# Routing in a fused decoder layer: its first two parts behind the mix and behind the next reciprocal, the ranking for blank entries at the heads of steps

## The chip, the cores and the metric

The kernel runs on one core of a Trainium2 chip. A core has five engines, each with an in-order queue of its own: TensorE (PE in the profile; PEld is its loading of weights), VectorE (DVE), ScalarE (ACT), GpSimd (POOL) and SyncE (SP, which here issues DMAs). They work side by side and wait for each other by semaphores. The metric is the device time of one execution in microseconds; of several runs the median is taken.

## The reference

The reference computes a decoder layer on 16 sequences of 128 rows of 256 numbers, in float32, and has three parts, each on a layer-normalised input and added to it.

```python
x = x + _L0_attn_ref(_layernorm(x), ...)                    # causal attention, 16 heads, latent size 72
x = x + _L0_xattn_ref(_layernorm(x), ctx, ctx, w, u)        # bidirectional decaying sums over ctx, gated by sigmoid(x)
x = x + _L0_ffn_ref(_layernorm(x), router_w, w_gate, w_up, w_down)   # 8 experts, two of them for each row
```

What matters here is how the third part chooses its experts for a row:

```python
logits = x @ router_w.T                     # 8 numbers a row
m1, ind1 = max(scores), argmax(scores)      # the best expert
m2, ind2 = the same with ind1 masked        # the second best
mult1, mult2 = softmax over those within the jitter threshold, at ind1 and ind2
out += dense_w[:, e] * ((silu(x @ w_gate[e].T) * (x @ w_up[e].T)) @ w_down[e].T)   # for each e
```

## The kernel before, in words

**Two halves.** The first 64 steps do attention, gating and routing; a step is one unit, four of the 16 heads of one sequence, so that a sequence `b` begins at step 4b. After them come 36 slots (`turn`, `up` L1033, `down` L1058, `add` L1071), each of which takes 128 listed rows through one expert; some of the slots stand under a condition. A slot gathers its rows by a list and adds its result into the output with an indirect DMA.

**A step.** The loop at the end of the function writes out the order of the work by hand: `scores` of unit s (L465) on TensorE; `normalize` of unit s-1, which is the reciprocal of the sums on VectorE (L502) and the product on GpSimd (L503); what the plan has for the place "pre"; `turn_probs` of unit s-2, four transposes on TensorE (L509) and a copy by ScalarE (L511); place "A"; `maxima` of unit s on VectorE (L482), its four exponentials on ScalarE (L490) and `lay_mask`, which writes the mask into the bank of scores that step s+2 will use (L477); the query tiles of the next pair of sequences (L427, with their copies by ScalarE L433 further down); place "B"; `values` (L517) and their copies (L529, L532); places "C" and "D". Within a place, what was entered first comes first. All engines are fed from this one order, each with its own share of it, and `ctx.enter_context(tc.manual_schedule())` keeps it as written.

**The plan.** `at(step, place, function, ...)` enters a piece of work. For each sequence it holds, beside others: `wkv_exps` (ScalarE L556 and L558, GpSimd L559 and L560), the two decaying sums (VectorE L568 and L585, with additions on GpSimd L580 and L590), `project` (TensorE L543), `residual` (VectorE L596), `mix_1` and `mix_2` (VectorE L625, the reciprocal L630 of 128x256, the product L631, then GpSimd's addition L632), the statistics of the mixed rows (L328, L329, L321, GpSimd L323), the normalised row (ScalarE L648), and the logits (TensorE L675, copied by VectorE L687). For most sequences the mix stands at place "B" of step 4b+9.

**PSUM.** Transposes share two banks under the tag "t": those of the probabilities L509, of the gating sums L621 (which the mix reads, L631 last), of rows and of latents. Query tiles, logits, the ranking of routing and the small products of the blank entries share two banks under "mm". A bank is free again when its last reader is done.

**Routing.** `route(r)` handles four sequences at once and is a generator; each `route_part` runs it to its next `yield`. The first part makes absolute values (VectorE L704) and finds the best expert (L707 a maximum, L709 and L710, L711 a maximum, L712, then L714 to mask it); the second part finds the second best by the same five instructions L707 to L712. The third takes the differences (L717 to L722, with an exponential on ScalarE, L723). The fourth ranks rows among those of the same expert by matmuls on TensorE (L728 to L731) and makes the gates (L739 to L741); the fifth makes the places (L754 to L765). The scatters of entries into lists by GpSimd (L771) follow.

**Blank entries.** For the first four sequences alone, `strangers` runs between the fifth part and the scatters. Its six parts are: two small VectorE instructions (L787, L788), two comparisons of 128x1024 (L793, a part for each), sixteen small matmuls on TensorE with their copy (L804, L808), a transpose with its copy (L812, L813), and a DMA by SP (L815). Entries of `lists` that no row takes have to name rows that are not of this expert, and this part finds them.

**Tables.** `first_table` counts the rows of each expert and makes a list of slots. Its first part is a product on TensorE (L823) and five small VectorE instructions (L825 to L835).

Of the kernel before, what the change touches and what calls it, by code (L numbers as in the profile page):

```python
# [19 lines left out]
B = 16  # L20
T = 128
N = B * T
C = 256
# [55 lines left out]
def decoder_kernel(  # L79
# [1004 lines left out]
    def at(step, place, fn, *args):  # L1084
        plan.setdefault((step, place), []).append((fn, args))
# [107 lines left out]
    for b in range(B):  # L1193
        s = NHG * b
        if b + 1 < B:
            at(s + 2, "pre", load_ctx, b + 1)
        at(s + 1, "C", wkv_exps, b)
        at(s + 2, "B", wkv_back, b)
        at(s + 3, "A", wkv_back_add, b)
        at(s + 4, "B", wkv_forth, b)  # L1200
        at(s + 5, "A", wkv_forth_add, b)
        at(s + 5, "B", project, b, (0, 1))
        at(s + 6, "B", project, b, (2, 3))
        at(s + 6, "C", rest_values, b)
        at(s + 7, "B", project, b, (4, 5))
        at(s + 7, "C" if b < B - 1 else "B", project, b, (6, 7, NP))
        for name, (step, place) in {B - 2: last_but_one, B - 1: last}.get(b, usual).items():
            at(s + step, place, stages[name], b)
        if b < E:
            for k in range(3):  # L1210
                at(s + 11 + k, "C", load_expert, b, k)
        if b % RB == RB - 1:
            r = b // RB
            parts = ((13, "B"), (13, "C"), (14, "B"), (15, "B"), (15, "C"))
            if b == B - 1:
                parts = ((12, "B"), (12, "D"), (13, "B"), (13, "D"), (14, "B"))
            for step, place in parts:
                at(s + step, place, route_part, r)
            if r == 0:
                for step, place in ((16, "B"), (16, "C"), (17, "B"), (17, "C"), (18, "C"), (19, "B")):  # L1220
                    at(s + step, place, route_part, r)
            for k in range(2 * RB):
                if b < B - 1:
                    at(s + (20 if r == 0 else 16) + k, "A", route_part, r)
                else:
                    at(s + 14 + (k + 1) // 3, "CDA"[(k + 2) % 3 if k > 1 else k], route_part, r)
        if b + 1 in FIRST_B:
            i = FIRST_B.index(b + 1)
            parts = [(19 + k, "C") for k in range(6)]
            if i:  # L1230
                parts = [(18, "C"), (20, "D"), (21, "B"), (21, "D"), (22, "D"), (23, "D")]
            for step, place in parts:
                at(s + step, place, table_part, i, first_table, i)
            for k in range(0, S1[i], 2):
                at(s + 24 + k // 2, "C", list_slots, min(2, S1[i] - k))
        if b == B - 1:
            for k in range(5):
                at(s + 15 + k // 3, "ABD"[k % 3], table_part, "2", last_table)
            for k in range(0, S2, 4):
                at(s + 17 + k // 4, "C", list_slots, min(4, S2 - k))  # L1240
# [153 lines left out]
```

## Time and profile before

| | |
|---|---|
| median of 3 runs | 553.93 us (552.38 to 557.51) |
| the profiled execution | 551.19 us |
| its span in the profile | 549.4 us |
| mean granted clock of TensorE | 0.989 |
| busy share of the span: PE, DVE, ACT, POOL | 93%, 60%, 60%, 60% |

The span runs from the first to the last instruction of the profiled execution; the rest of its time lies around it. The busy shares are averages over two halves that differ: in the steps all four engines have work, in the slots nearly everything waits for TensorE. A row of the timeline has the start in us, the duration in us, the engine, the line, the operation, what is written from what, the sizes and the number of instructions; in brackets stands how long the engine had been idle and whose end released it. A row of stretches has the bounds in us, the length, the busy time of PE, PEld, DVE, ACT and POOL with the number of instructions, the granted clock, the busy share of the DMA engines and GB/s.

### The profile page before, as it was taken

To read this page: it belongs to the slowest core of one execution; us is meant where nothing else is said; L and a number is where in the kernel's file an instruction comes from. 1 tells how busy PE (TensorE), PEld (TensorE's weight loads), DVE (VectorE), ACT (ScalarE), POOL (GpSimd) and SP (SyncE) were. 2 spreads that over 40 slices of the span, in tenths; PEclk is the share of its full clock that TensorE was granted. 3 is DMA by queue.
4 is the path that set the end of the run, shared out by engine and by line. 5 is a ranking of instruction groups with operands and counts; after the bars stand their busy time and mean duration, and the time that the engine had idled before them with its cause. 6 is when DMAs were issued, how large, how long until landed. Compare 5 with 4: busy or idle time off the path is not lost. (4 is left out here: it accounts for less than half of the span.)

```text
span 549.4 us, 10171 instructions
## 1 busy us (share of the span) xinstructions
PE 512.7 (93%) x3289; PEld 438.4 (80%) x3289; DVE 330.0 (60%) x811; ACT 329.3 (60%) x953; POOL 330.9 (60%) x386
## 2 busy tenths in 40 slices
PE   4999999999989999999998989999989999998991
PEld 3778788877768876887875769989979999997991
DVE  2345676677986687888859867565654333333320
ACT  1788998898788897888887873523422222222210
POOL 5456656574576985687655895555685454543522
PEclk9899999999999999999998999999999999999997
DMA  5422255363453555222131122233223423232221
GB/s 150 110 79 69 66 143 175 115 192 125 109 182 118 157 142 158 81 69 67 32 100 36 52 55 55 49 61 45 43 39 53 59 41 56 41 53 47 39 30 19
DMA packets 39632, 45.51 MB, mean 83 GB/s; under 512 B 14129, under 2 KB 31410, under 8 KB 39578
## 3 DMA queue, kind: packets, MB, share of 16 engines
q1 hardware_dynamic: 30076, 35.12, 22.5%
q0 software_dynamic: 7936, 9.51, 11.3%
q8 instruction: 28, 0.46, 0.4%
q10 hardware_dynamic: 1566, 0.21, 0.2%
q14 instruction: 26, 0.21, 0.2%
HBM read 26.12 MB, written 11.23 MB: 68 GB/s over the span
## 5 line engine op out<-in xcount | busy, mean ns | idle before, releaser
L1071 POOL DMA_INDIRECT out_dram<-y,en x36 | 62.0, 1724 | 78.9 <-DVE y L1069 54.6
L490 ACT ACTIVATE pr<-s,nm 128x128 f32<-128x128 f32 x256 | 90.7, 370 | 11.4 <-DVE nm L482 11.3
L503 POOL TENSOR_TENSOR pr<-pr,rsum 128x512 f32<-128x512 f32 x64 | 75.7, 1183 | 36.0 <-DVE rsum L502 23.8
L1046 ACT ACTIVATE sl<-s 128x512 f32<-128x512 f32 x36 | 21.5, 597 | 119.0 <-PE s L1033 107.3
L465 PEld LDWEIGHTS s<-kvT,q 72*128 72x128 f32 x512 | 65.8, 192 | 16.6 <-issue 12.1
L1033 PEld LDWEIGHTS s<-xT,w 128*128 128x128 f32 x576 | 69.2, 192 | 9.5 <-issue 6.8
L1033 PE MATMUL s<-xT,w 128*128 128x128 f32 x576 | 70.8, 276 | 5.1 <-DVEq L1019 2.0
L543 PE MATMUL po<-outw_sb,yP 128*128 128x256 f32 x288 | 74.1, 385 | 0.7 <-DMA yP<-yd 0.7
L465 PE MATMUL s<-kvT,q 72*128 72x128 f32 x512 | 70.2, 279 | 1.9 <-DMA q<-qr 1.7
L1048 DVE TENSOR_TENSOR hT<-sl,pu 128x512 f32<-128x512 f32 x36 | 24.7, 687 | 76.2 <-PE pu L1033 57.1
L1033 PE MATMUL pu<-xT,w 128*128 128x128 f32 x576 | 70.2, 275 | 0.0
L1058 PE MATMUL pd<-wall,hT 128*128 x288 | 68.2, 380 | 0.8 <-DVE hT L1048 0.8
L517 PE MATMUL py<-aT,kvN 128*72 128x512 f32 x128 | 66.3, 600 | 1.6 <-ACT aT L511 1.3
L1033 PEld LDWEIGHTS pu<-xT,w 128*128 128x128 f32 x576 | 67.3, 192 | 0.1
L427 PE MATMUL pq<-xnT,wq_sb 128*128 128x256 f32 x256 | 65.8, 389 | 0.6 <-DVE found L808 0.6
L543 PEld LDWEIGHTS po<-outw_sb,yP 128*128 128x128 f32 x288 | 54.1, 193 | 12.7 <-issue 5.2
L482 DVE TENSOR_REDUCE nm<-s 128x4 f32<-128x512 f32 x64 | 43.7, 682 | 27.6 <-PE s L465 26.8
L1058 PEld LDWEIGHTS pd<-wall,hT 128*128 128x128 f32 x288 | 51.9, 190 | 6.6 <-DVE hT L1048 1.0
L511 ACT COPY aT<-pt 128x512 f32<-128x512 f32 x64 | 37.2, 582 | 27.6 <-PE pt L509 26.8
L490 ACT ACTIVATION_READ_ACCUMULATOR pr<-s,nm 128x1 f32 x256 | 53.1, 207 | 0.0
L427 PEld LDWEIGHTS pq<-xnT,wq_sb 128*128 128x128 f32 x256 | 46.0, 195 | 6.0 <-DVE found L808 1.0
L966 POOL DMA_INDIRECT xr<-xn,en x36 | 37.4, 1040 | 14.1 <-issue 7.7
(182 smaller groups left out, 870.1 us busy)
## 6 DMA issues: line engine op xcount, KB each, us to landing
wall<-in_wg_dram SPq DMA_DIRECT2D x8, 512.0 KB
wall<-in_wu_dram SPq DMA_DIRECT2D x8, 512.0 KB
wall<-in_wd_dram SPq DMA_DIRECT2D x8, 512.0 KB
q<-q SPq DMA_DIRECT2D x16, 224.0 KB
yP<-yB SPq DMA_DIRECT2D x32, 112.0 KB
cx<-in_cx_dram SPq DMA_DIRECT2D x16, 128.0 KB
out_dram<-x SPq DMA_DIRECT2D x16, 128.0 KB
xn<-row SPq DMA_DIRECT2D x16, 128.0 KB
```

The source lines that it names most:

```text
L427: nc.tensor.matmul(pq[:, :GT], w[:, c, :], xnT[g][:, c, :], start=(c == 0), stop=(c == NC - 1))
L465: nc.tensor.matmul(ps[:, j, :], q[g, hg][0:L, j, ts(i, T)], kvT[g][:, ts(i, T)], start=False, stop=(j == HG - 1), skip_group_check=n >= 2,)
L482: nc.vector.tensor_reduce(nm, ps, AX.X, ALU.max, negate=True)
L490: nc.scalar.activation(pr[:, j, :], ps[:, j, :], AF.Exp, bias=nm[:, j : j + 1], accum_out=sums[:, j : j + 1],)
L503: nc.gpsimd.tensor_mul(pr, pr, rsum.unsqueeze(2).to_broadcast([P, HG, T]))
L511: nc.scalar.copy(aT, pt)
L517: nc.tensor.matmul(py[:L], kvN[g][:, ts(i, L)], aTs.pop((b, hg)), start=True, stop=True)
L543: nc.tensor.matmul(pos[b][:, :C], yP[b][:, i, :], outw_sb[:, i, :], start=(i == 0), stop=(i == NP))
L966: nc.gpsimd.indirect_dma_start(out=xr, out_offset=None, in_=xn2[0 : t["rows"], :], in_offset=bass.IndirectOffsetOnAxis(ap=entries[j][:, 0: ...
L1033: nc.tensor.matmul(o[:, ts(f, P)], w[:, c * F + f * P : c * F + (f + 1) * P], xT[:, c, :], start=(c == 0), stop=(c == NC - 1),)
L1058: nc.tensor.matmul(pd[:, :C], hT[:, f, :], wall[:, bass.ds(e, 1), WD0 + f * C : WD0 + (f + 1) * C], start=(f == 0), stop=(f == NF - 1),)
L1071: nc.gpsimd.indirect_dma_start(out=out2, out_offset=bass.IndirectOffsetOnAxis(ap=en[:, 1:2], axis=0), in_=y, in_offset=None, compute_op=AL ...
```

## The change

Only steps and places in the plan change.

```diff
         if b % RB == RB - 1:
             r = b // RB
-            parts = ((13, "B"), (13, "C"), (14, "B"), (15, "B"), (15, "C"))
+            parts = ((13, "C"), (14, "pre"), (14, "B"), (15, "B"), (15, "C"))
             if b == B - 1:
                 parts = ((12, "B"), (12, "D"), (13, "B"), (13, "D"), (14, "B"))
             for step, place in parts:
                 at(s + step, place, route_part, r)
             if r == 0:
-                for step, place in ((16, "B"), (16, "C"), (17, "B"), (17, "C"), (18, "C"), (19, "B")):
+                for step, place in ((16, "B"), (17, "pre"), (18, "pre"), (18, "A"), (19, "A"), (19, "B")):
                     at(s + step, place, route_part, r)
...
             parts = [(19 + k, "C") for k in range(6)]
             if i:
-                parts = [(18, "C"), (20, "D"), (21, "B"), (21, "D"), (22, "D"), (23, "D")]
+                parts = [(19, "pre"), (20, "D"), (21, "B"), (21, "D"), (22, "D"), (23, "D")]
```

Here `s` is 4b. For the first three routings (b = 3, 7, 11) the first part moves from place "B" to place "C" of step s+13, which is step 25, 41 and 57: on VectorE it stood ahead of the mix of sequence b+1, which is in place "B" of the same step, and stands behind it now. The second part moves from place "C" to "pre" of the next step, behind the reciprocal L502 with which `normalize` opens that step. The fourth routing is as it was.

For the blank entries (b = 3) the first comparison moves from place "C" of step 28 to "pre" of step 29, the second from "B" of step 29 to "pre" of step 30; the small matmuls move from "C" of step 29 to "A" of step 30, behind the transposes of that step and ahead of its query tiles, and the transpose from "C" of step 30 to "A" of step 31. The first part and the DMA keep their places.

The first part of the second table moves from "C" of step 62 to "pre" of step 63.

No instruction, DMA or buffer is added or removed; GpSimd's and SP's queues keep their order.

## The prediction

> **What bounds the kernel.** I read the page first. TensorE is busy nearly all of the time, so a microsecond counts only where TensorE waits.
>
> ```profile
> PE 512.7 (93%) x3289; PEld 438.4 (80%) x3289; DVE 330.0 (60%) x811; ACT 329.3 (60%) x953; POOL 330.9 (60%) x386
> ```
>
> Then I took TensorE's rows of the timeline, cut them at the scores (L465) that open each step, and summed the idle time inside. Steps 3 to 25, 31 to 39 and most later ones have none: such steps take 4 to 6 us. The waits lie where routing is. Step 26 begins at 134.85, step 27 at 139.68; this is the timeline around them.
>
> ```profile
> 136.06 0.42 DVE L631 TENSOR_TENSOR r<-pw,r 128x256 f32<-128x256 f32 x1
> ...
> 136.63 0.77 POOL L632 TENSOR_TENSOR x<-x,r 128x256 f32<-128x256 f32 x1 [4.15 <-DVE m L707]
> 136.63 0.63 PE L509 MATMUL pt<-ident,pr 128*128 128x128 f32 x4 [0.68 <-DVE m L707]
> 136.84 0.60 DVE L710 TENSOR_TENSOR oh<-oh,rev 128x32 f32<-128x32 f32 x1
> ...
> 138.33 0.68 DVE L482 TENSOR_REDUCE nm<-s 128x4 f32<-128x512 f32 x1
> ...
> 139.04 0.37 ACT L490 ACTIVATE pr<-s,nm 128x128 f32<-128x128 f32 x1 [1.16 <-DVE nm L482]
> ...
> 141.73 0.47 ACT L433 ACTIVATE q<-pq,bq_sb 128x256 f32<-128x256 f32 x1
> ...
> 142.25 0.41 PE L728 MATMUL pf<-sel,before 128*128 128x32 f32 x2 [0.21 <-ACT q L433]
> ```
>
> Two waits to see. The transposes L509 wait 0.68 us: they need the PSUM bank that L631, the mix's last product, frees at 136.48 (the profile names the next DVE instruction, L707). Then the ranking L728 waits for L433, which frees its PSUM bank. L433 stands at the end of an unbroken ScalarE chain (four exponentials, mask, two copies) that began at 139.04, when DVE's maxima L482 were done. DVE has no gap from 131.89 to 143.0. **So in steps 25 to 27 DVE's queue up to L482 sets when TensorE passes L728**; 0.68 us saved before that is returned there. The second routing (steps 41 to 43) repeats it: 0.72 and 0.21 us. The third (57 to 59) has no query tiles beside it:
>
> ```profile
> 296.68 0.66 PE L509 MATMUL pt<-ident,pr 128*128 128x128 f32 x4 [1.51 <-POOL pr L503]
> ...
> 294.70:298.11 3.41, 1.90 (x19) 1.71 (x17) 3.31 (x13) 2.42 (x11) 1.98 (x4) 1.00 0.28 85
> 298.11:301.52 3.41, 3.41 (x9) 2.17 (x9) 3.34 (x8) 2.51 (x11) 3.41 (x5) 0.50 0.00 0
> ```
>
> The last two rows are stretches; the seventh number is the granted clock. After 3.41 us with 1.90 us of TensorE work, the next 3.41 us ran at 0.50. The blank-entry part costs two waits in step 30:
>
> ```profile
> 152.36 1.73 DVE L793 TENSOR_TENSOR wall<-pf,wall 128x1024 bf16<-128x1024 f32 x1
> ...
> 158.07 1.13 PE L427 MATMUL pq<-xnT,wq_sb 128*128 128x256 f32 x4 [0.63 <-DVE found L808]
> ...
> 161.96 0.27 PE L812 MATMUL strangers_t<-ident,found 128*8 128x128 f32 x1 [1.04 <-ACT q L433]
> ```
>
> **Routing's first two parts (three times).** No instruction is added or removed, and no DMA moves; DVE's order alone changes. DVE must still do the same list before L482: mix, both parts, the reciprocal L502. If nothing else changed, L482 would come when it does now. What changes is beside what on GpSimd the list lies. The row above shows the price: L710 takes 0.60 us instead of its usual 0.19 because GpSimd's L632 runs until 137.40; L712 likewise waits for L559 (0.43 instead of 0.19). L707 and L711, reductions of one operand, keep 0.18 and 0.19 beside the same GpSimd work, and so does L502. So DVE instructions with two SBUF operands wait for GpSimd's running one. The first part has five (L704, L709, L710, L712, L714), and today, at 132.50 to 133.91, no GpSimd instruction stands beside them. Behind the mix they meet L632, which L631 releases, then L559 and L560; the second part, behind L502, meets L503 (1.04 us), which L502 releases.
>
> Worked with the starts and durations of the rows (GpSimd starts 0.15 us after its releaser ends; a waiting DVE instruction ends 0.04 us after GpSimd's; L559 is held by ScalarE's L556, done at 136.18):
>
> | instruction | before | after |
> |---|---|---|
> | L625 mix | 133.82 | 132.50 |
> | L631 ends | 136.48 | 135.16 |
> | L632 GpSimd | 136.63 | 135.31 |
> | first part | 132.50-133.91 | 135.08-137.85 |
> | L502 | 138.05 | 137.78 |
> | L503 GpSimd | 138.72 | 138.09 |
> | second part | 136.40-138.13 | 137.86-139.65 |
> | L482 | 138.33 | 139.78 |
>
> Waits in the new order: L709 0.54 for L632, L712 0.30 for L559, L714 0.48 for L560, the second L710 0.77 for L503: 2.09 us. In the old order, ahead of L482: 0.41 + 0.24 = 0.65. So L482 comes 1.45 us later; the wait of L717 behind it (0.89 instead of 0.18) goes, but no one on TensorE's path gains from that. Behind L482 on ScalarE are queued the exponentials, mask, and L433; L728 follows at 143.7 instead of 142.25, and TensorE has no idle time in steps 28 and 29 to return it: **+1.45 us**. The second routing gives **+1.4** (L482 from 218.21 to 219.6). Bounds: at best no wait at all, -0.65; at worst every two-operand instruction is caught once more, +1.7. I take the worked value because each wait copies a row.
>
> Third routing: the mix starts at 288.82 instead of 290.66, L502 comes at 294.0 instead of 294.88, L503 ends near 295.5, and the 1.51 us wait shrinks to some 0.4. But L482 goes from 294.97 to 295.9, ScalarE's copy L511 to 299.3, and L517 to 299.9 instead of 300.16. The cold stretch mostly vanishes, so step 60 could start 0.9 earlier; yet DVE, busy throughout, reaches the residual L596 only at 303.1 instead of 303.19, and step 61's copy of probabilities follows 0.3 earlier. **-0.3**, between 0 and -1.0.
>
> [...] There L543 x4 and L517 x2 took 1.85 and 1.54 us start to start instead of 0.87 and 0.86: **1.66 us**. [...] The stretches lie on a grid of 3.41 us; from 141.4 to 144.9 the new order has no wide matmul, so a grid stretch almost empty of them is met with about 0.4 chance (starts from 140.7 to 142.1). The second routing lies 79.87 us or 23.4 grid steps later, so its chance is nearly the complement: I count one cold stretch, **+1.66**; none and two are the bounds.
>
> **The blank entries.** The first L793 goes behind L502 of its step, the second behind the next L502, so the mix L625 starts at 152.4 instead of 154.01. Then the second L793 ends at 157.5, and TensorE, in whose queue the sixteen L804 stand right behind L509, waits from 156.1 to 157.6: 1.5 us, in place of 0.63 + 1.04; queries and L543 are queued behind. L812, now a step later, finds its bank free. L465 of step 31 comes 0.6 earlier, L482 of step 31 0.3 later (DVE waits for L812 ahead of L813), step 32 0.35 earlier: **-0.35**, between -1.7 (both waits gone) and +1.7 (a cold stretch). SP's store of the blanks slips about a us; the GpSimd scatters that follow it begin 7 us behind.
>
> **The second table's first part** (five DVE instructions of 0.2 us, step 62 to 63): L502 gets ahead of it, but L503 stands on GpSimd behind L771, L966 and L323 until 318.62 anyway. 0, within 0.4.
>
> **Sum.** 1.45 + 1.4 - 0.3 - 0.35 + 1.66 = +3.9 us. The profiled execution took 551.19 (span 549.4), 2.74 under the median of the runs shown, 553.93. I lay the sum on both: 555.1 for a profiled one like it, 557.8 for the median.
>
> **Rivals.**
> - *More cold stretches*, chance 0.33: both routings or the blanks' wait chill the clock; +5.5 to +7.5, 560 to 561. For: gaps of 2.3 us twice and 1.5 once, against the one of 1.51 that did it. Against: another stretch, 410.75 to 414.16, with 2.14 us of work, cost nothing. It decides once two of them fall badly.
> - *The locks but no cold stretch*, 0.11: +2.2, 556.1.
> - *The gaps close*, 0.10, the one on the other side: TensorE's waits for L631, L503 and L793 go and the DVE instructions slip between GpSimd's. Then L482 comes 0.65 earlier twice, the third routing gives 1.0, the blanks 1.76: -4.1, 549.9. It decides if L482 ends before 139.0, that is if DVE's waits ahead of it sum to under 0.65. For: L709 did slip 0.02 us ahead of L632. Against: in the new order it is 0.08 us behind.
> - *Nothing*, 0.08: gains and losses cancel, 553.9.
> The forecast, one cold stretch, has 0.38: 557.8, itself between 556 and 560.
>
> A measurement of this kernel tells about 1% from no change, 5.5 us. Slower by more: the 0.33 and a quarter of the forecast's, 0.42. Faster by more (below 548.4): half of the closing gaps, 0.05. Within: 0.53. The range leaves out the ends of both outer rivals: 552.0 to 562.5.
>
> **What the profile would show.** Right: L509 of step 26 without a wait, L709, L712 and L714 of the first part at 0.4 to 0.7 us, L482 about 2.0 us behind the start of L502 instead of 0.3, and a wait of 2 us before L728; a row of clock at 0.5 near 145 or 225; 1.5 us before L804. Wrong: L728 with under 0.9 us of wait, or L482 no later than before against the mix's start.

## The result, and the profile after

The changed kernel takes 560.19 us (median of 4 runs, 559.22 to 564.08), the kernel before beside it 555.67 (median of 4); the ratio is 1.0127, with a 95% interval of 1.0085 to 1.0170. It is a ratio of the fast runs alone, and so not that of the two medians, which is 1.0081. In a later group of runs (after_again below) it is 1.0096, from 1.0063 to 1.0129. So the changed kernel is about 1% slower. The profiled execution took 559.22 us instead of 551.19, its span 557.4 instead of 549.4.

This is the timeline of the changed kernel around the first routing, the rows that answer to those shown of before. Counted from the scores L465, step 25 begins at 131.72, step 26 at 135.85 and step 27 at 139.82.

```profile
132.90 0.69 DVE L482 TENSOR_REDUCE nm<-s 128x4 f32<-128x512 f32 x1 [0.83 <-PE s L465]
...
135.74 0.42 DVE L631 TENSOR_TENSOR r<-pw,r 128x256 f32<-128x256 f32 x1
...
136.31 0.73 POOL L632 TENSOR_TENSOR x<-x,r 128x256 f32<-128x256 f32 x1 [2.82 <-DVE r L631]
136.39 0.69 DVE L709 TENSOR_TENSOR oh<-src,m 128x32 f32<-128x32 f32 x1
...
136.79 0.60 PE L509 MATMUL pt<-ident,pr 128*128 128x128 f32 x4
...
137.12 0.19 DVE L710 TENSOR_TENSOR oh<-oh,rev 128x32 f32<-128x32 f32 x1
...
137.26 0.72 POOL L559 TENSOR_TENSOR kv<-kv,cx 128x256 f32<-128x256 f32 x1 [0.22 <-ACT kv L556]
...
137.57 0.47 DVE L712 TENSOR_TENSOR oh<-oh,first 128x32 f32<-128x32 f32 x1
...
137.94 0.72 POOL L560 TENSOR_TENSOR S<-S,cx 128x256 f32<-128x256 f32 x1
...
138.07 0.65 DVE L714 SCALAR_TENSOR_TENSOR src<-oh,src 128x32 f32<-128x32 f32 x1
138.64 0.16 DVE L502 RECIPROCAL rsum<-sums 128x4 f32<-128x4 f32 x1
138.88 1.04 POOL L503 TENSOR_TENSOR pr<-pr,rsum 128x512 f32<-128x512 f32 x1 [0.21 <-DVE rsum L502]
138.97 1.00 DVE L709 TENSOR_TENSOR oh<-src,m 128x32 f32<-128x32 f32 x1
...
140.78 0.68 DVE L482 TENSOR_REDUCE nm<-s 128x4 f32<-128x512 f32 x1
...
141.49 0.37 ACT L490 ACTIVATE pr<-s,nm 128x128 f32<-128x128 f32 x1 [3.25 <-DVE nm L482]
...
144.70 0.41 PE L728 MATMUL pf<-sel,before 128*128 128x32 f32 x2 [2.52 <-ACT q L433]
```

The wait before L509 is gone, and a wait of 2.52 us before L728 stands in its place. VectorE's L709, L712, L714 and the second L709 take 0.69, 0.47, 0.65 and 1.00 us instead of 0.19; each ends about 0.05 us behind the GpSimd instruction beside it (L632, L559, L560, L503). L710 at 137.12 slips in ahead of L559 and keeps 0.19. The stretches of the same kernel (bounds, length, busy PE, PEld, DVE, ACT and POOL, granted clock, DMA share, GB/s) show what follows:

```profile
143.11:146.52 3.41, 1.82 (x13) 1.77 (x14) 2.12 (x5) 3.40 (x13) 3.41 (x5) 1.00 0.03 8
146.52:149.94 3.42, 3.42 (x7) 1.83 (x7) 1.65 (x12) 1.56 (x4) 1.46 (x5) 0.50 0.00 0
225.03:228.44 3.41, 0.89 (x9) 0.81 (x8) 3.34 (x8) 3.38 (x14) 2.46 (x3) 1.00 0.07 21
228.44:231.86 3.42, 3.42 (x11) 2.36 (x11) 2.08 (x12) 1.59 (x7) 2.22 (x6) 0.50 0.02 5
306.95:310.36 3.41, 3.32 (x6) 1.93 (x7) 2.88 (x13) 3.14 (x12) 2.21 (x7) 0.50 0.00 0
```

A stretch at a granted clock of 0.50 is called cold here. There are three, one behind each of the three routings; before had only one behind a routing, the third, and one among its first steps, at 21.63. Both also end cold (from 543.87 and from 549.30), behind their last matmuls. Where the 8.0 us of span lie, by the starts of L465:

| steps | before | after | difference |
|---|---|---|---|
| start of the span to step 25 | 130.72 | 131.72 | +1.0 |
| 25 to 28, first routing | 15.77 | 18.90 | +3.1 |
| 28 to 32, blank entries | 21.24 | 20.97 | -0.3 |
| 32 to 41 | 42.82 | 43.06 | +0.2 |
| 41 to 44, second routing | 15.82 | 18.89 | +3.1 |
| 44 to 57 | 60.68 | 60.66 | 0.0 |
| 57 to 61, third routing | 19.84 | 20.56 | +0.7 |
| 61 to the end | 242.52 | 242.66 | +0.1 |

The 1.0 us at the start lies ahead of all that was changed: the first sixteen matmuls of L427 take 5.19 us instead of 4.32, and other small waits differ.

### The profile page after: what moved, and what is told of

The parts are those of the page before. It is cut to its first block, busy times and chain, and to the rows that moved or that the text cites. A ratio compares the mean times of both kernels' runs of the same rounds, so it can differ in the third digit from the quotient of the medians.

```text
span 557.4 us, 10171 instructions
## 1 busy us (share of the span) xinstructions
PE 515.9 (93%) x3289; PEld 439.7 (79%) x3289; DVE 329.8 (59%) x811; ACT 328.3 (59%) x953; POOL 332.4 (60%) x386
## 5 line engine op out<-in xcount | busy, mean ns | idle before, releaser
L503 POOL TENSOR_TENSOR pr<-pr,rsum 128x512 f32<-128x512 f32 x64 | 75.4, 1178 | 35.7 <-DVE rsum L502 27.5
L465 PEld LDWEIGHTS s<-kvT,q 72*128 72x128 f32 x512 | 65.9, 191 | 19.6 <-issue 13.7
L543 PE MATMUL po<-outw_sb,yP 128*128 128x256 f32 x288 | 76.0, 392 | 0.7 <-DMA yP<-yd 0.7
L465 PE MATMUL s<-kvT,q 72*128 72x128 f32 x512 | 70.3, 279 | 3.1 <-DMA q<-qr 2.1
L517 PE MATMUL py<-aT,kvN 128*72 128x512 f32 x128 | 68.0, 614 | 2.5 <-ACT aT L511 2.2
L543 PEld LDWEIGHTS po<-outw_sb,yP 128*128 128x128 f32 x288 | 55.2, 197 | 14.5 <-issue 6.5
L427 PE MATMUL pq<-xnT,wq_sb 128*128 128x256 f32 x256 | 65.5, 388 | 0.0
L482 DVE TENSOR_REDUCE nm<-s 128x4 f32<-128x512 f32 x64 | 43.7, 683 | 28.2 <-PE s L465 28.2
L427 PEld LDWEIGHTS pq<-xnT,wq_sb 128*128 128x128 f32 x256 | 46.1, 195 | 5.2 <-ACT q L433 0.3
```

The lines of the kernel that those rows point to most:

```text
L427: nc.tensor.matmul(pq[:, :GT], w[:, c, :], xnT[g][:, c, :], start=(c == 0), stop=(c == NC - 1))
L465: nc.tensor.matmul(ps[:, j, :], q[g, hg][0:L, j, ts(i, T)], kvT[g][:, ts(i, T)], start=False, stop=(j == HG - 1), skip_group_check=n >= 2,)
L482: nc.vector.tensor_reduce(nm, ps, AX.X, ALU.max, negate=True)
L503: nc.gpsimd.tensor_mul(pr, pr, rsum.unsqueeze(2).to_broadcast([P, HG, T]))
L517: nc.tensor.matmul(py[:L], kvN[g][:, ts(i, L)], aTs.pop((b, hg)), start=True, stop=True)
L543: nc.tensor.matmul(pos[b][:, :C], yP[b][:, i, :], outw_sb[:, i, :], start=(i == 0), stop=(i == NP))
```

## The experiments

"Before" was run again beside each group, so that its median differs from group to group; ratios are to it, with 95% intervals. Each kernel left one profiled execution, from which its waits and stretches are read.

**Which part carries the loss?** Routing alone:

```diff
-            parts = ((13, "B"), (13, "C"), (14, "B"), (15, "B"), (15, "C"))
+            parts = ((13, "C"), (14, "pre"), (14, "B"), (15, "B"), (15, "C"))
```

> Only the three routings' first and second parts are moved; blank entries and the table stay as before. Theory (DVE's two-operand instructions wait for GpSimd, so the maxima L482 of steps 26, 42 and 58 come late, ScalarE's chain and the ranking L728 with them, and the emptied stretch of TensorE turns the clock cold): steps 25 to 27 and 41 to 43 get longer by 3.1 us each as in the changed kernel, a wait of 2.5 us before L728 twice, a cold stretch after each; +6 to +8 us in all, as slow as the changed kernel or 0.3 us slower. Rival (the move of the blank entries carries the loss): within 1 us of before.

Measured: 559.97 us, ratio 1.0168 (1.0138 to 1.0199). The wait before L728 is 2.52 us twice; steps 25 to 28 take 20.52 us and 41 to 44 20.57, some 1.65 more each than in the changed kernel, as behind each wait the clock stood at 0.50 for two stretches on end:

```profile
141.17:144.58 3.41, 0.93 (x5) 0.48 (x3) 3.31 (x13) 3.13 (x13) 1.60 (x2) 1.00 0.35 115
144.58:151.41 6.83, 6.79 (x19) 5.03 (x20) 2.00 (x14) 3.27 (x12) 3.33 (x7) 0.50 0.00 0
```

Blank entries and table alone:

```diff
-                for step, place in ((16, "B"), (16, "C"), (17, "B"), (17, "C"), (18, "C"), (19, "B")):
+                for step, place in ((16, "B"), (17, "pre"), (18, "pre"), (18, "A"), (19, "A"), (19, "B")):
...
-                parts = [(18, "C"), (20, "D"), (21, "B"), (21, "D"), (22, "D"), (23, "D")]
+                parts = [(19, "pre"), (20, "D"), (21, "B"), (21, "D"), (22, "D"), (23, "D")]
```

> Only the blank entries and the second table's first part are moved; routing stays as before. Theory: the wait before L804 (1.5 us) takes the place of those before L427 and L812 (0.63 and 1.04), -0.3 us; within 1 us of before unless the clock turns cold there (+1.7). Rival (the blank entries carry the loss): +5 us or more.

Measured: 551.60 us, ratio 1.0009 (0.9990 to 1.0027). In the profiled execution the wait before L804 is 1.46 us, a cold stretch followed it, and steps 28 to 32 take 22.66 us; in the changed kernel, with the same wait and no cold stretch there, they take 20.97. Behind the third routing, where before had its cold stretch, this execution had none: steps 57 to 61 take 18.54 us instead of 19.84. The move of the blank entries is worth nothing that can be measured; routing carries all of the loss.

**Do GpSimd's instructions set the delay?** GpSimd's reading work beside the moved parts is left out or replaced by fills with zeros:

```diff
-        nc.gpsimd.tensor_mul(kv[:, :, 0, :], kv[:, :, 1, :], v)
-        nc.gpsimd.tensor_mul(s[:, :, 0, :], s[:, :, 1, :], v)
+        if b in (6, 10, 14):
+            nc.gpsimd.memset(kv[:, :, 0, :], 0.0)
+            nc.gpsimd.memset(s[:, :, 0, :], 0.0)
+        else:
+            nc.gpsimd.tensor_mul(kv[:, :, 0, :], kv[:, :, 1, :], v)
+            nc.gpsimd.tensor_mul(s[:, :, 0, :], s[:, :, 1, :], v)
...
-        nc.gpsimd.tensor_add(xs[b], xs[b], r)
+        if b not in (4, 8, 12):
+            nc.gpsimd.tensor_add(xs[b], xs[b], r)
...
-        nc.gpsimd.tensor_mul(pr, pr, rsum.unsqueeze(2).to_broadcast([P, HG, T]))
+        if (b, hg) not in ((6, 1), (10, 1), (14, 1)):
+            nc.gpsimd.tensor_mul(pr, pr, rsum.unsqueeze(2).to_broadcast([P, HG, T]))
```

> The changed kernel, but GpSimd has no reading work beside the moved parts: it leaves out the addition L632 of sequences 4, 8 and 12, the product L503 of units 25, 41 and 57, and fills the numerators of L559 and L560 of sequences 6, 10 and 14 with zeros instead of multiplying. Theory (the locks set the delay): L709, L712, L714 take 0.19 us, L482 starts about 1.2 us behind the start of L502 instead of 2.0, 2.2 to 2.8 us earlier in all, the wait before L728 falls from 2.5 to under 0.6 us, and no cold stretch follows steps 27 and 43. Rival (the order itself, or waits for semaphores between the parts, sets the delay): DVE's instructions keep their length and L728 waits over 2 us.

Measured: one run of 546.87 us. Its code has six more lines, so that L709, L712, L714 and L728 stand as L715, L718, L720 and L734 in its timeline:

```profile
135.75 0.19 DVE L715 TENSOR_TENSOR oh<-src,m 128x32 f32<-128x32 f32 x1
...
136.42 0.19 DVE L718 TENSOR_TENSOR oh<-oh,first 128x32 f32<-128x32 f32 x1
136.65 0.19 DVE L720 SCALAR_TENSOR_TENSOR src<-oh,src 128x32 f32<-128x32 f32 x1
136.76 0.17 DVE L502 RECIPROCAL rsum<-sums 128x4 f32<-128x4 f32 x1
...
138.10 0.68 DVE L482 TENSOR_REDUCE nm<-s 128x4 f32<-128x512 f32 x1
...
142.01 0.41 PE L734 MATMUL pf<-sel,before 128*128 128x32 f32 x2 [0.48 <-ACT q L433]
```

Same order, same twelve instructions, and none of them waits: L482 stands 1.34 us behind the start of L502 instead of 2.14, the wait before the ranking is 0.48 us, and steps 25 to 28 take 15.17 us with no cold stretch. This shows that the waits for GpSimd's running instructions (called locks in the prediction and the expectations), and not the order as such, make the delay.

**Which of the two moves?** The first part alone behind the mix, the second following it ahead of L502:

```diff
-            parts = ((13, "B"), (13, "C"), (14, "B"), (15, "B"), (15, "C"))
+            parts = ((13, "C"), (13, "C"), (14, "B"), (15, "B"), (15, "C"))
```

> Only the first part of the three routings is moved, behind the mix; the second follows it, still ahead of the reciprocal L502; the rest as before. Theory: L709, L712 and L714 of the first part wait 0.5 us each for L632, L559 and L560, the second part meets no GpSimd work because L503 waits for L502, so L482 comes 0.7 to 0.8 us later than before instead of 1.5; the wait before L728 is 1.6 to 1.8 us instead of 2.5, 2 to 5 us more than before according to how many cold stretches follow. Rival (the second part behind L502 does all the harm): within 1 us of before or faster.

Measured: 554.91 us, ratio 1.0037 (1.0019 to 1.0055). The first part's L709, L712 and L714 wait as in the changed kernel (0.69, 0.47 and 0.65 us), the second part's L709 takes 0.19. The wait before L728 is 1.33 us, less than expected, and one of 0.23 stands before L509 of the same step; no cold stretch followed, and steps 25 to 28 take 16.48 us, 0.7 more than before.

The second part alone behind L502:

```diff
-            parts = ((13, "B"), (13, "C"), (14, "B"), (15, "B"), (15, "C"))
+            parts = ((13, "B"), (14, "pre"), (14, "B"), (15, "B"), (15, "C"))
```

> Only the second part of the three routings is moved, behind L502; the first stays ahead of the mix; the rest as before. Theory: the second part meets L632, L559 and L560, L482 comes 0.6 to 0.7 us later than before, the wait of 0.68 us before L509 stays and the one before L728 grows from 0.21 to 0.9: 1 to 3 us more than before. Rival (the first part behind the mix does all the harm): within 1 us of before.

Measured: 553.16 us, ratio 1.0013 (0.9986 to 1.0040), which by itself doesn't tell it from before: the whole is where the rival had it. Its timeline shows the loss:

```profile
137.53 0.63 PE L509 MATMUL pt<-ident,pr 128*128 128x128 f32 x4 [0.67 <-DVE rsum L502]
137.57 0.73 DVE L709 TENSOR_TENSOR oh<-src,m 128x32 f32<-128x32 f32 x1
138.34 0.65 DVE L710 TENSOR_TENSOR oh<-oh,rev 128x32 f32<-128x32 f32 x1
...
143.74 0.41 PE L728 MATMUL pf<-sel,before 128*128 128x32 f32 x2 [0.79 <-ACT q L433]
```

The wait before L509 stays and the one before L728 grows from 0.21 to 0.79; steps 25 to 28 take 16.35 us, 0.6 more than before. Each move alone costs 0.6 to 0.7 us a routing, together 1.4, and only the two together empty TensorE for 2.5 us.

The changed kernel beside these:

> The changed kernel itself, on the same chip as these three, to see how many cold stretches it has in another execution. Theory: two waits of 2.5 us before L728, a cold stretch after at least one of them, 5 to 9 us more than before.

Measured: 558.32 us, ratio 1.0096 (1.0063 to 1.0129); the wait of 2.52 us twice, a cold stretch behind the first and two behind the second.

**Does the clock turn cold because TensorE stands empty?** The changed kernel, with the wait filled:

```diff
         made = [(n, t, *query_tile(n, t)) for n, t in tiles[:2]]
+        if s in (27, 43):
+            (n, t, pq, _), = made
+            for c in 2 * tuple(range(NC)):
+                nc.tensor.matmul(
+                    pq[:, :GT], wq_sb[:, :, t, 0:P][:, c, :], xnT[n][:, c, :], start=(c == 0), stop=(c == NC - 1)
+                )
```

> The changed kernel, with the query tile of steps 27 and 43 multiplied three times instead of once, which puts 1.7 us of wide matmuls into the wait before L728 and changes no result. Theory (the cold stretch follows from the emptied TensorE): no cold row after steps 27 and 43, L728 at the same time as in the changed kernel, 2 x 1.66 = 3.3 us less than the changed kernel. Rival (the clock turns cold by itself, by heat or load or chance): the cold rows stay, and the time is that of the changed kernel or 3.5 us longer where the filling is on the path.

Measured: 554.96 us, ratio 1.0064 (1.0035 to 1.0094), against 1.0127 and 1.0096 of the changed kernel. The timeline around the filled wait:

```profile
143.39 1.89 PE L1314 MATMUL pq<-xnT,wq_sb 128*128 128x256 f32 x8
146.08 0.41 PE L728 MATMUL pf<-sel,before 128*128 128x32 f32 x2 [0.80 <-ACT q L433]
```

And the stretches there:

```profile
142.64:146.06 3.42, 2.64 (x13) 1.98 (x11) 3.32 (x13) 3.16 (x13) 1.64 (x2) 1.00 0.38 123
146.06:149.47 3.41, 3.39 (x19) 2.67 (x20) 1.94 (x12) 2.67 (x11) 2.26 (x6) 1.00 0.00 0
```

Redundant work that changes no result made these steps faster: L728 stands 12.99 us behind the scores of step 25 as in the changed kernel (12.98), but the clock stays at 1.00, and steps 25 to 28 and 41 to 44 take 17.22 us each instead of 18.9. That is 1.68 us a stretch. For the whole kernel the gain isn't shown as clearly: its interval overlaps those of the changed kernel, and its profiled execution had cold stretches elsewhere, among them one behind the blank entries' wait, where the changed kernel had none (steps 28 to 32 take 22.62 us instead of 20.97). The ten runs of this kernel fall into two groups, 551.3 to 553.8 and 556.1 to 557.3, in turn; why is open.

**A version that keeps routing behind L482.** All parts of the first three routings go behind the maxima of their step, one part a step:

```diff
-            parts = ((13, "B"), (13, "C"), (14, "B"), (15, "B"), (15, "C"))
+            parts = ((14, "C"), (15, "C"), (16, "C"), (17, "C"), (18, "B"))
...
-                for step, place in ((16, "B"), (16, "C"), (17, "B"), (17, "C"), (18, "C"), (19, "B")):
+                for step, place in ((18, "C"), (19, "B"), (20, "B"), (21, "A"), (22, "A"), (22, "B")):
...
-                    at(s + (20 if r == 0 else 16) + k, "A", route_part, r)
+                    at(s + (23 + k if r == 0 else 19 + k // 2), "A", route_part, r)
```

> Routing's parts all go behind the maxima, one part a step: first part at place C of step 4b+14, second at C of 4b+15, third at C of 4b+16, ranking at C of 4b+17, places at B of 4b+18; the blank entries follow from C of step 30 to B of step 34, the scatters start up to three steps later (two a step for the second and third routing). Theory (what counts is what DVE must do ahead of L482): the mix is followed by L502 and L482 directly, so no wait before L509 and L728 in steps 25 to 28 and 41 to 44, none of 1.5 us in step 59, none before L804 and L812, no cold stretch in the middle: 3 to 6 us less than before, about 546 where before takes 551. Rival (routing costs DVE and TensorE the same wherever it stands): within 1 us of before.

Measured: 550.23 us, ratio 0.9966 (0.9946 to 0.9985): faster than before, by 2 us, less than expected. Steps 25 to 28 have no wait, and L482 waits for TensorE now and not TensorE for it:

```profile
135.65 0.17 DVE L502 RECIPROCAL rsum<-sums 128x4 f32<-128x4 f32 x1
136.56 0.69 DVE L482 TENSOR_REDUCE nm<-s 128x4 f32<-128x512 f32 x1 [0.55 <-PE s L465]
...
142.84 0.95 DVE L709 TENSOR_TENSOR oh<-src,m 128x32 f32<-128x32 f32 x1
```

L709 of the second part still waits 0.76 us for GpSimd's L503, but nothing that TensorE needs stands behind it. What was missing of the gain: the counts of the second table, L823 in step 62, wait 1.74 us for the third routing's places, which stand later now, and a cold stretch begins behind that wait, at 312.30; and there are 0.64 and 0.26 us of waits in steps 32 and 33.

The same version with the first part of the second table one step later:

```diff
-                parts = [(18, "C"), (20, "D"), (21, "B"), (21, "D"), (22, "D"), (23, "D")]
+                parts = [(19, "C"), (20, "D"), (21, "B"), (21, "D"), (22, "D"), (23, "D")]
```

> As e7_behind, but the second table's first part stands at place C of step 63 instead of 62, behind the places of the third routing that it counts. Theory: the wait of 1.74 us before L823 in step 62 goes and with it 1 to 1.7 us of the steps 61 to 63; no other wait comes in its place, so the whole is 0.6 to 0.8 per cent faster than before. Rival (scatters and table at the end of the steps are held by GpSimd and DVE in any case, and the slots start no earlier): no faster than e7_behind, 0.3 per cent faster than before.

Measured: 548.92 us where before takes 550.42, ratio 0.9970 (0.9946 to 0.9995). The wait of 1.74 us is gone and steps 61 to 63 take 7.64 us instead of 9.80, but the whole is no faster than the version ahead of it, as its rival had it. Its profiled execution has two cold stretches elsewhere (at 173.58 and 327.18), and steps 32 to 41, where the first one lies, take 1.43 us more than in e7_behind. Whether such stretches ate the 2 us in the other runs too, or the rival's reason holds, is not known.

## Why the prediction was right or wrong, point by point

The first point below needs one more row of before, the maxima of step 25, and the third point three rows of its stretch at 0.50 (298.11 to 301.52):

```profile
131.89 0.69 DVE L482 TENSOR_REDUCE nm<-s 128x4 f32<-128x512 f32 x1 [0.83 <-PE s L465]
...
298.31 2.06 PE L543 MATMUL po<-outw_sb,yP 128*128 128x256 f32 x4
300.16 1.71 PE L517 MATMUL py<-aT,kvN 128*72 128x512 f32 x2
301.70 1.46 PE L543 MATMUL po<-outw_sb,yP 128*128 128x256 f32 x6
```

- **VectorE's list ahead of L482 sets L728: right.** From L482 of step 25 to that of step 26 it was 6.44 us before (131.89 to 138.33) and is 7.88 after (132.90 to 140.78): +1.44, forecast +1.45. The waits by name are L709 0.50, L712 0.28, L714 0.46 and, of the second part, 0.81: 2.05, forecast 2.09. The last one caught L709 where the prediction had L710, which changes nothing. One reading was off: L707 of before ended at 136.57, ahead of L632's start at 136.63, so it doesn't show that one-operand instructions keep their time beside GpSimd; L711 (0.19 us at 137.47, beside L559) and L502 (0.17 at 138.05, beside L560) do. e6_no_gpsimd shows the cause.
- **The wait before L728: right.** 2.52 us, forecast about 2.3. Steps 25 to 28 gained 3.13 and 41 to 44 3.07 us; forecast were 1.45 and 1.4 with 1.66 for each that turns cold.
- **That the wait before L728 can cost a stretch of the clock: right.** The prediction's case for it was the wait of 1.51 us in step 59 of before, behind which the clock stood at 0.50 for 3.41 us. With 2.52 us each of the first two routings was followed by a cold stretch (from 146.52 and from 228.44), and with the wait filled (e3_fill) the same steps stayed at 1.00. The 1.66 us for a stretch are from the rows above: L543 x4 and L517 x2 took 1.85 and 1.54 us from start to start there instead of 0.87 and 0.86. The filling saved 1.68 us a stretch.
- **"I count one cold stretch": wrong, and this is the step that failed.** Both of the first two routings were followed by one, in all three profiled executions that have both moves and no filling (here, after_again, e1_routing), and in three of these six cases it was twice as long. What was mis-sized is the chance of "about 0.4" for each routing. It held that a stretch of the grid has to begin 1.6 to 3.0 us ahead of L728 (at 140.7 to 142.1, for an L728 at 143.7). In the six cases the stretch that turned the next one cold began 1.59 and 2.60 us ahead of L728 here, 2.13 and 3.40 in after_again, 3.45 and 3.08 in e1_routing. So starts over at least 1.86 us were followed by one, more than half of a grid step, and none of the six was spared; the three that lie clearly outside the forecast's limit are those with the double stretch. Why the limit is so much wider stays open.
- **"Its chance is nearly the complement": wrong too, but it doesn't explain the second stretch.** The spacing of the two routings came from the trace of before, 79.87 us or 23.4 grid steps. The first routing's delay and its cold stretch, 3.1 us, lie between the two: the step that holds L728 begins at 139.82 and 222.74, which is 82.92 us or 24.3 grid steps. But the spacing only says how the two chances hang together. With 0.4 for each, 0.8 cold stretches are to be expected whatever the spacing is.
- **The third routing, forecast -0.3: wrong in the profiled execution, +0.7.** The wait before L509 fell from 1.51 to under 0.1, and waits of 0.77 before L728 and 0.95 before L517 took its place. What was wrong is "the cold stretch mostly vanishes": one came all the same, behind both of these waits here, and behind the one of 0.77 alone in after_again and e1_routing. There it began 3.4 and 3.5 us behind the scores of step 59 instead of 5.7, and steps 57 to 61 took 19.43 and 19.49 us, 0.4 less than before, near the forecast though the cold stretch stayed: in part luck.
- **The blank entries: right.** 1.46 us before L804 (forecast 1.5), steps 28 to 32 shorter by 0.27 (forecast 0.35). That no cold stretch followed is luck: the same wait was followed by one in e2_blanks and e3_fill, where these steps are 1.4 us longer than before, inside the bound of +1.7. The second table: no change, as forecast.
- **The sum.** +3.9 was forecast, with "within 1%" likeliest and slower next. With one more cold stretch, 1.66, and the third routing's 1.0 it is +6.6; the rest of the 8.0 us of the profiled execution, 1.0 at the start and some tenths, is not of the change. The medians lie less far apart than this pair of executions, 4.5 us here and 5.9 in after_again, so that the +3.9 is nearer to them than to the 8.0. Executions of one kernel differ in their cold stretches, as their clocks say: the mean granted clock of the runs of after_again lies between 0.982 and 0.989, that of before beside them between 0.982 and 0.993, and one stretch of 3.41 us at half clock in 557 takes 0.003. What the profiles show is the first rival, more cold stretches.

## What to carry to other kernels

Before you move work on an engine to fill a gap, list what that engine must finish ahead of the next result that another engine waits for: an order that closes one wait but leaves the list as long moves the wait to the next hand-over (here 0.68 us before L509 and 0.21 before L728 became 2.52 before L728). Look, too, at what GpSimd runs beside the moved VectorE instructions; here the same twelve instructions took 2.5 us without GpSimd's reads beside them (e6_no_gpsimd: 1.40 + 1.08) and 4.5 with them (changed kernel: 2.64 + 1.89). Work that no one waits for soon belongs behind the result that the bound engine needs, not just ahead of it.

When a wait on TensorE grows, ask what it does to the clock after it. A limit for that taken from one cold stretch in one trace is too weak to count stretches with (here a chance of 0.4 against six cold stretches behind six waits); and when one delay can move the next, don't take the spacing from the old trace.

## What the runs showed of the hardware

- Cold stretches by the wait ahead of them, in these executions: of 2.52 us, six of six were followed by one, three of the six by one twice as long (6.83 us); of 1.33 and 1.34 in e4_first, none of two; of 1.43 to 1.51, the clock turned cold in step 59 of before and of e5_second and in step 30 of e2_blanks, e3_fill and e6_no_gpsimd, and stayed at 1.00 in step 30 of the changed kernel and of after_again and in step 59 of e2_blanks. In before a cold stretch began at 21.63 behind waits of 0.50 and 0.17 us only, and in e8_table_later one at 173.58 behind 0.64 and 0.26. So the longest gap alone doesn't decide. Nor does TensorE's busy time in the stretch ahead: 2.50 us in before (18.22 to 21.63) and 2.25 in the changed kernel (303.54 to 306.95) were followed by a cold stretch, while 2.13 in before (410.75 to 414.16) and 1.68 in the changed kernel (501.49 to 504.90) were not. What decides stays open.
- In the changed kernel the cold stretches begin 24 steps of 3.41 us apart (146.52 to 228.44) and 23 (from there to 306.95), in before 81 (21.63 to 298.11).
- A few multiplications done again for nothing made steps 25 to 28 and 41 to 44 of the changed kernel 1.68 us faster each, as with 1.7 us of filling the 3.41 us from 146.06 stayed at a clock of 1.00 (e3_fill).
- In e6_no_gpsimd GpSimd ran nothing at all beside the moved parts: it had been idle for 6.90 us when its L323 began at 140.37. So that run sets its reading work against none; what fills with zeros would cost there was not tried.
